# Layer 3 of a conv/attention hybrid: the output bias as a GpSimd addition to T

## The chip, the core and the metric

The kernel runs on one core of a Trainium2 chip. It is one program of 192724 instructions. Five engines work side by side: TensorE (PE; its weight loads are listed as PEld), VectorE (DVE), ScalarE (ACT), GpSimd (POOL) and SyncE (SP), which here issues most DMAs. Each takes its instructions in order, and they wait for each other through semaphores. The metric is the time of one execution on the device, in microseconds (us).

## What is computed

The input x is (4, 128, 48, 48): four images of 2304 positions and 128 channels. Five layers of work follow: a selective-scan block (layer 0), a deformable convolution (layer 1), a stack of linear attention with an expert layer (layer 2), and causal attention with another expert layer (layer 3). The change lies in the causal attention of layer 3:

```
t = _to_tokens(x)                       # (4, 2304, 128)
...
t = t + _L3_attn_ref(_ln_t(t), ...)
t = t + _L3_ffn_ref(_ln_t(t), ...)

def _L3_attn_ref(x, qkv_w, qkv_b, out_w, out_b):     # 4 heads of 32
    qkv = jnp.einsum('btc,oc->bto', x, qkv_w) + qkv_b
    q, k, v = jnp.split(qkv, 3, axis=-1)
    ...
    att = jnp.where(causal, att, -jnp.inf)
    att = jax.nn.softmax(att, axis=-1)
    out = jnp.einsum('bhqk,bhkd->bhqd', att, v)
    ...
    return jnp.einsum('btc,oc->bto', out, out_w) + out_b
```

The bias that concerns us is `out_b`, plus the part of the value bias that passes through the output weights: since the weights of a softmax sum to one, the bias of v adds `v_b @ out_w.T` to every row. The kernel forms this sum once, in `o_b`.

## The kernel before

T holds the tokens of all images in on-chip memory, [128 partitions, 4 x 18 tiles, 128 channels] in f32, and stays there from layer 1 to the end. A tile is 128 tokens; a block is three tiles (384 tokens), so an image has six blocks. The four heads are worked in two pairs, so layer 3 has 4 x 6 x 2 = 48 pieces of work, called `Block` in the code.

For each image, `normed` takes mean and variance of all 18 tiles (VectorE) and turns the variance into a factor (GpSimd, L1817). For each of its blocks, `prepare` returns seven steps: `norm` writes the normalised block xn (three VectorE instructions, L1830); `turn` transposes it (TensorE, L1842) and copies it to xT (ACT, L1844); four `project` steps make q and k for two pairs of heads (L1848, then VectorE L1854 or ACT L1850); `value` makes v (L1866, ACT L1869). `largest` takes the row maxima of the scores: score products on TensorE (L1891), on the diagonal an addition (L1900), then the maximum on VectorE (L1901); `take` transposes the maxima (L1910) and adds them to q (L1912). `scores` makes one tile row of transposed scores (L1945), its exponential on ACT (L1953), and on the last three rows of a block the causal mask on GpSimd (L1956); `weighed` multiplies it with v (L1974), three units later (UNIT_LAG). When both pairs of a block are done, `divide` runs in six steps: two empty ones, the reciprocal in two halves and the product with it (L1999, L2001), an empty one, and `output`, whose inner function `project` multiplies with the output weights (L1925), adds the bias (L1926) and adds the result to T (VectorE, L1928).

The order on TensorE, ACT, VectorE and GpSimd is the order in which the Python code calls these steps: the whole layer stands under `manual_schedule`. The main loop goes through the 48 blocks and their tile rows. In each unit it calls `scores`, then as many steps of `largest` for the following block as are due, then one step of `divide` if any is waiting (`doing`), then, in every other unit or in short blocks in each, one step of preparation (`others`), and then `weighed` for the unit three back.

Results of TensorE go to PSUM. The pool `ps` has one buffer with the tag "ps" for the transposes, q, k, v, the maxima and the output projection, so each of these waits until the one before it has been read. The scores for the maxima have one buffer too (`pa`), the transposed scores two (`pb`), the weighted sums one (`po`).

A row of ones (`env.ones_row`, one partition of 128) as weights, times a row of 128 values, writes these values to all 128 partitions. This is how L1926 adds the bias: a product with a single row behind each projection product, three times per block, into the same PSUM tile.

A similar bias addition exists in layer 2: there GpSimd adds a bias tile to three tiles of tokens (L1180), and the tile is made by one product with the row of ones and a copy.

Of the kernel before, what the change touches and what calls it, by code (L numbers as in the profile page):

```python
# [15 lines left out]
F32 = mybir.dt.float32  # L16
# [7 lines left out]
P = 128  # L24
NB = 4
C = 128
# [5 lines left out]
G3 = BLK // P  # L32
# [1715 lines left out]
def layer3(env, io, T):  # L1748

    with ExitStack() as ctx:  # L1750
        _layer3(ctx, env, io, T)
# [5 lines left out]
def _layer3(ctx, env, io, T):  # L1757
# [6 lines left out]
    nc, tc, ident = env.nc, env.tc, env.ident  # L1764
    cp = ctx.enter_context(tc.tile_pool(name="l3c", bufs=1))
# [7 lines left out]
    def load(name, shape):  # L1773
        t = cp.tile(shape, F32, name=name)
        nc.sync.dma_start(t, io[name])
        return t

    def psum(*shape):
        return ps.tile(list(shape), F32, name="ps", tag="ps")
# [4 lines left out]
    v_b = load("l3_v_b", [P, 1])  # L1784
    oT_w = load("l3_owT", [P, C])
    o_b = load("l3_ob", [1, C])
    later = load("l3_later", [P, P])

    spread = [cp.tile([P, G3, P], F32, name=f"spread{i}") for i in range(NP3)]
# [11 lines left out]
    def normed(im):  # L1801

        t = {}

        def some(g0):
            if g0 == 0:
                t["st"] = sp.tile([P, NT, nc.vector.BN_STATS_DIM], F32, name="st")
                im.mv = sp.tile([P, NT, nc.vector.BN_AGGR_DIM], F32, name="mv")
                im.rstd = sp.tile([P, NT], F32, name="rstd")
                im.q = bp.tile([P, NP3, L], F32, name="q")  # L1810
                im.k = bp.tile([P, NP3, L], F32, name="k")
            for g in range(g0, g0 + G3):
                nc.vector.bn_stats(out=t["st"][:, g, :], in_=im.T[:, g, :])
                nc.vector.bn_aggr(out=im.mv[:, g, :], in_=t["st"][:, g, :])
            if g0 + G3 == NT:
                nc.vector.tensor_scalar_add(im.rstd, im.mv[:, :, 1], 1e-5)
                nc.gpsimd.tensor_tensor(im.rstd, im.rstd, env.half[:, :NT], ALU.pow)  # L1817

        return [lambda g0=g0: some(g0) for g0 in range(0, NT, G3)]

    def prepare(im, j):

        at = bass.ts(j, BLK)
        t = {}

        def norm():
            t["xn"] = sp.tile([P, G3, C], F32, name="xn")
            for g in range(G3):
                i = j * G3 + g
                nc.vector.tensor_scalar(  # L1830
                    t["xn"][:, g, :],
                    im.T[:, i, :],
                    im.mv[:, i, 0:1],
                    im.rstd[:, i : i + 1],
                    op0=ALU.subtract,
                    op1=ALU.mult,
                )

        def turn():
            pt = psum(P, BLK)  # L1840
            for g in range(G3):
                nc.tensor.transpose(pt[:, bass.ts(g, P)], t["xn"][:, g, :], ident)  # L1842
            t["xT"] = sp.tile([P, BLK], F32, name="xT")
            nc.scalar.copy(t["xT"], pt)  # L1844

        def project(s, p):
            pq = psum(P, BLK)
            nc.tensor.matmul(pq, w_qk[:, s, p, :], t["xT"], start=True, stop=True)  # L1848
            if s:
                nc.scalar.activation(  # L1850
                    im.k[:, p, at], pq, AF.Identity, bias=b_qk[:, s, p : p + 1]
                )
            else:
                nc.vector.tensor_scalar(  # L1854
                    im.q[:, p, at],
                    pq,
                    b_qk[:, s, p : p + 1],
                    DH3**-0.5,
                    op0=ALU.add,
                    op1=ALU.mult,  # L1860
                )

        def value():
            pv = psum(P, G3, C)
            for g in range(G3):
                nc.tensor.matmul(  # L1866
                    pv[:, g, :], t["xT"][:, bass.ts(g, P)], w_v, start=True, stop=True
                )
            nc.scalar.copy(  # L1869
                im.v[:, j * G3 : (j + 1) * G3, :, :DH3],  # L1870
                pv.rearrange("p g (h d) -> p g h d", d=DH3),
            )

        return [norm, turn] + [
            lambda s=s, p=p: project(s, p) for s in range(2) for p in range(NP3)
        ] + [value]
# [44 lines left out]
    def output(im, j, oT):  # L1921
        def project():
            pp = psum(P, G3, C)
            for g in range(G3):
                nc.tensor.matmul(pp[:, g, :], oT[:, bass.ts(g, P)], oT_w, start=True, stop=False)  # L1925
                nc.tensor.matmul(pp[:, g, :], env.ones_row, o_b, start=False, stop=True)  # L1926
            dst = im.T[:, j * G3 : (j + 1) * G3, :]
            nc.vector.tensor_add(dst, dst, pp)  # L1928

        return project  # L1930
# [8 lines left out]
    def scores(x, t):  # L1939
        g0 = max(t - x.j * G3, 0)  # L1940
        cols = slice(g0 * P, BLK)
        sc = pb.tile([P, 2, 512], F32, name="scT")
        for r in range(2):
            rows = slice(r * 64, r * 64 + 64)
            nc.tensor.matmul(  # L1945
                sc[:, r, cols],
                x.im.k[rows, x.p, bass.ts(t, P)],
                x.im.q[rows, x.p, x.j * BLK + g0 * P : (x.j + 1) * BLK],
                start=True,
                stop=True,  # L1950
            )
        pT = sp.tile([P, 2, BLK], F32, name="pT", bufs=UNIT_LAG + 2)
        nc.scalar.activation(pT[:, :, cols], sc[:, :, cols], AF.Exp)  # L1953
        if t >= x.j * G3:
            own = pT[:, :, g0 * P : (g0 + 1) * P]
            nc.gpsimd.affine_select(  # L1956
                out=own,
                in_=own,
                pattern=[[0, 2], [1, P]],
                compare_op=ALU.is_ge,  # L1960
                fill=0.0,
                base=0,
                channel_multiplier=-1,
            )
        x.__dict__.setdefault("pT", {})[t] = pT
# [54 lines left out]
    def preparation(im):  # L2020
        return normed(im) + [s for j in range(NBLK) for s in prepare(im, j)]

    def run(steps):
        for s in steps:
            s()

    with tc.manual_schedule(engines=ORDERED):
        pr = psum(1, C)
        nc.tensor.matmul(pr, v_b, oT_w, start=True, stop=True)
        nc.vector.tensor_add(o_b, o_b, pr)  # L2030
        run(normed(images[0]) + prepare(images[0], 0))
        parts, take = largest(images[0], 0, 0)
        run(parts + [take])
        others = [s for j in range(1, NBLK) for s in prepare(images[0], j)]
        waiting, done, doing = [], [], []
        for i, x in enumerate(blocks):
            n = x.last + 1
            if x.j == 0 and x.p == 0 and x.im.b + 1 < NB:
                others += preparation(images[x.im.b + 1])
            following = blocks[i + 1] if i + 1 < len(blocks) else None  # L2040
            parts, take = largest(following.im, following.j, following.p) if following else ([], None)
            if following and following.im is x.im and x.im.b == 0:

                need = (NBLK - 1 - following.j) * (2 + 2 * NP3 + 1)
                need += 0 if x.im.b + 1 == NB else len(preparation(images[1]))
                while len(others) > need:
                    others.pop(0)()
            total = len(parts)
            for t in range(n):
                scores(x, t)  # L2050
                while parts and (total - len(parts)) * max(n - 1, 1) < total * (t + 1):
                    parts.pop(0)()
                if doing:
                    doing.pop(0)()
                if others and (t % 2 == 0 or n < 7):
                    others.pop(0)()
                waiting.append((x, t))
                if len(waiting) > UNIT_LAG:
                    y, s = waiting.pop(0)
                    weighed(y, s)  # L2060
                    if s == y.last and y.p == NP3 - 1:
                        doing += divide(y)
            run(parts)
            if following and following.im is not x.im:
                run(others)
                others = []
            if take:
                take()
        for y, s in waiting:
            weighed(y, s)  # L2070
            if s == y.last and y.p == NP3 - 1:
                doing += divide(y)
        run(doing)
# [155 lines left out]
```

## Time and profile before

| | |
|---|---|
| time, median of 3 runs | 12985.0 us (12982.07 to 13003.0) |
| profiled execution | 12885.25 us |
| its span (first to last instruction) | 12883.3 us |
| TensorE busy | 11151.3 us (87%) |
| VectorE busy | 8493.7 us (66%) |
| ACT busy | 6929.4 us (54%) |
| GpSimd busy | 4401.5 us (34%) |
| layer 3, from its first product to its last addition to T | 11028 to 12565 us |
| mean granted clock of TensorE | 0.935 |

How to read it: the profile lists each engine's instructions grouped by the line of the kernel that issued them and by operation. Each group gives what it writes and reads, partitions x elements, how many there are, their busy time and mean duration, and how long the engine sat idle just before them and for whom it waited. Matrix products of f32 operands are recorded as two instructions each. Products overlap in the pipeline, so that the duration of one is longer than the distance from its start to the next one's. The granted clock is the share of its full clock that TensorE was given.

### The profile page before, as it was taken

To read this page: it belongs to the slowest core of one execution; us is meant where nothing else is said; L and a number is where in the kernel's file an instruction comes from. 1 tells how busy PE (TensorE), PEld (TensorE's weight loads), DVE (VectorE), ACT (ScalarE), POOL (GpSimd) and SP (SyncE) were. 2 spreads that over 40 slices of the span, in tenths; PEclk is the share of its full clock that TensorE was granted. 3 is DMA by queue.
4 is the path that set the end of the run, shared out by engine and by line. 5 is a ranking of instruction groups with operands and counts; after the bars stand their busy time and mean duration, and the time that the engine had idled before them with its cause. 6 is when DMAs were issued, how large, how long until landed. Compare 5 with 4: busy or idle time off the path is not lost. (4 is left out here: it accounts for less than half of the span.)

```text
span 12883.3 us, 192724 instructions
## 1 busy us (share of the span) xinstructions
PE 11151.3 (87%) x71150; PEld 8431.5 (65%) x71150; DVE 8493.7 (66%) x15424; ACT 6929.4 (54%) x13281; POOL 4401.5 (34%) x4727
## 2 busy tenths in 40 slices
PE   6879788878797887689799999999999997899997
PEld 4667666766676666488677787777877774333333
DVE  4998889888988899455555666566665653444442
ACT  3777777777777777311155655555565653123322
POOL 1443333333333344277643333333333331000000
PEclk9999999999999999799899999999999997799995
DMA  2221222122212222266500000000000003000003
GB/s 104 67 71 63 77 79 71 63 77 80 71 63 75 81 67 67 85 189 197 149 1 3 3 4 2 4 3 3 4 2 3 1 1 117 10 6 7 7 8 120
DMA packets 307846, 677.49 MB, mean 53 GB/s; under 512 B 39109, under 2 KB 128985, under 8 KB 304865
## 3 DMA queue, kind: packets, MB, share of 16 engines
q1 hardware_dynamic: 254032, 493.49, 12.2%
q0 software_dynamic: 51840, 169.91, 4.7%
q8 instruction: 571, 9.36, 0.3%
q14 instruction: 363, 2.97, 0.1%
q10 hardware_dynamic: 1040, 1.77, 0.0%
HBM read 602.63 MB, written 71.85 MB: 52 GB/s over the span
## 5 line engine op out<-in xcount | busy, mean ns | idle before, releaser
L565 ACT ACTIVATE hs<-ps,bct 128x256 f32<-128x256 f32 x4608 | 1853.9, 474 | 1182.0 <-PE ps L559 1130.5
L559 PE MATMUL ps<-ident,h 128*128 128x128 f32 x9216 | 1496.1, 294 | 778.8 <-DVE h L545 608.8
L559 PEld LDWEIGHTS ps<-ident,h 128*128 128x128 f32 x9216 | 1083.0, 148 | 1162.5 <-DVE h L545 716.2
L573 PE MATMUL yp<-ident,hs 128*128 128x128 f32 x9216 | 1408.2, 289 | 28.5 <-ACT ys L588 28.5
L505 ACT ACTIVATE dA<-delta,l_Al 128x768 f32<-128x768 f32 x1536 | 1388.3, 936 | 0.3
L512 POOL TENSOR_TENSOR h<-du,rB 128x512 f32<-128x512 f32 x768 | 1077.5, 1403 | 767.5 <-PE ps L559 689.0
L573 PEld LDWEIGHTS yp<-ident,hs 128*128 128x128 f32 x9216 | 1159.9, 151 | 82.7 <-ACT ys L588 57.6
L545 DVE TENSOR_TENSOR_SCAN h<-dA,h 128x256 f32<-128x256 f32 (+1 forms) x1024 | 1083.4, 1058 | 27.2
L545 DVE TENSOR_TENSOR_SCAN h<-dA,carry,h 128x768 f32<-128x768 f32 x512 | 1027.9, 2008 | 10.6 <-ACT dA L505 10.6
L1180 POOL TENSOR_TENSOR T<-T,bias 128x384 f32<-128x384 f32 x384 | 383.8, 999 | 1560.4 <-DVE fn L1108 1520.2
L487 POOL TENSOR_SCALAR_AFFINE_SELECT dB<-bct 128x512 f32<-128x512 f32 x768 | 748.4, 975 | 385.5 <-PE b L519 244.9
L1953 ACT ACTIVATE pT<-scT 128x768 f32<-128x768 f32 (+2 forms) x504 | 377.6, 749 | 894.2 <-PE scT L1945 894.0
L519 PE MATMUL b<-dB,duT 128*128 128x128 f32 x6144 | 830.2, 279 | 0.8 <-ACT duT L445 0.8
L545 DVE TENSOR_TENSOR_SCAN h<-dA,carry,b 128x512 f32<-128x512 f32 x512 | 645.7, 1261 | 267.8 <-PE b L519 250.5
L949 POOL DMA_INDIRECT g<-table,idx x648 | 710.1, 1096 | 263.6 <-issue 146.4
L519 PEld LDWEIGHTS b<-dB,duT 128*128 128x128 f32 x6144 | 770.7, 197 | 2.4 <-POOL h L512 1.2
L962 PE MATMUL pt<-ident,gw 128*128 128x128 f32 x5184 | 661.9, 283 | 103.3 <-DVE gw L956 100.4
L956 DVE TENSOR_TENSOR gw<-g,wq 128x512 f32<-128x512 f32 x648 | 445.9, 694 | 427.9 <-DMA g<-table,idx 377.3
L962 PEld LDWEIGHTS pt<-ident,gw 128*128 128x128 f32 x5184 | 608.0, 193 | 152.1 <-DVE gw L956 119.7
L552 POOL COPY carry<-h 128x2 f32<-128x2 f32 x512 | 97.3, 190 | 1780.4 <-DVE h L545 1715.2
L1901 DVE TENSOR_REDUCE mx<-sc 128x2 f32<-128x1024 f32 (+3 forms) x400 | 428.5, 1071 | 364.8 <-PE sc L1891 359.8
L516 DVE TENSOR_TENSOR h<-du,rB 128x512 f32<-128x512 f32 x768 | 633.3, 825 | 4.2 <-DMA rB<-rows 4.1
(341 smaller groups left out, 23182.1 us busy)
## 6 DMA issues: line engine op xcount, KB each, us to landing
rB<-rows SPq DMA_DIRECT2D x768, 384.0 KB, 3.5
w<-f_w SPq DMA_DIRECT2D x64, 1024.0 KB, 6.4
table<-y SPq DMA_DIRECT2D x9, 2304.0 KB, 17.8
table<-tok SPq DMA_DIRECT2D x16, 1152.0 KB, 10.4
g<-table,idx POOLq DMA_INDIRECT x648, 3.8
xb<-x SPq DMA_DIRECT2D x48, 192.0 KB, 3.1
xn<-xn SPq DMA_DIRECT2D x48, 192.0 KB, 3.5
yd<-y SPq DMA_DIRECT2D x4, 2304.0 KB
```

What stands on the lines that cost most here:

```text
L487: nc.gpsimd.affine_select(out=x.dB[n], in_=x.bc[:, m0 : m0 + CT // P, n : n + 1].to_broadcast([P, CT // P, P]), pattern=[[0, CT // P], [1, ...
L505: nc.scalar.activation(dA, x.delta[:, d, :], AF.Exp, scale=A[:, d, x.k, n : n + 1])
L512: nc.gpsimd.tensor_mul(h[:, 1, own], x.du[:, 1, own], x.rB[n][:, own])
L516: nc.vector.tensor_mul(x.h[n][:, :, own], x.du[:, :, own], b)
L519: nc.tensor.matmul(b0[:, bass.ts(m, P)], x.duT[:, m, :], x.dB[n][:, m, :], start=True, stop=True,)
L545: nc.vector.tensor_tensor_scan(h, da, b, initial=first, op0=ALU.mult, op1=ALU.add)
L559: nc.tensor.transpose(tt[:, m, bass.ts(d, P)], x.h[n][:, d, bass.ts(2 * q + m, P)], ident)
L565: nc.scalar.activation(hs, tt[:, m, :], AF.Copy, scale=x.bc[:, 2 * q + m, NS + n : NS + n + 1])
L573: nc.tensor.matmul(yp[:, q, (2 * d + m) * P : (2 * d + m + 1) * P], hs[:, bass.ts(d, P)], ident, is_transpose=True, start=n == 0 and m == ...
L949: nc.gpsimd.indirect_dma_start(out=g, out_offset=None, in_=table, in_offset=bass.IndirectOffsetOnAxis(ap=idx[:, j : j + 1], axis=0),)
L956: nc.vector.tensor_mul(gw, g.rearrange("p (q c) -> p q c", c=C), wq[:, i, t, :].unsqueeze(2).to_broadcast([P, 4, C]),)
L962: nc.tensor.matmul(pt[:, t - t0, :], gw[:, q, :], ident, start=q == 0, stop=q == 3)
```

## The change

The 72 products with the row of ones behind the output projection go. In their place, a tile `bias` of [128, 1, 128] is filled once at the start of layer 3 (one product with the row of ones, one ACT copy), and the step `turn` of each block begins with a GpSimd addition of this tile, repeated three times, to the block's own tiles of T. The block's norm (step `norm`) has read T by then; the attention's result is added to the same tiles later, in `project`.

```diff
@@ constants of layer 3
     o_b = load("l3_ob", [1, C])
+    bias = cp.tile([P, 1, C], F32, name="bias")
     later = load("l3_later", [P, P])
@@ prepare
         def turn():
+
+            own = im.T[:, j * G3 : (j + 1) * G3, :]
+            nc.gpsimd.tensor_add(own, own, bias.to_broadcast([P, G3, C]))
             pt = psum(P, BLK)
             for g in range(G3):
                 nc.tensor.transpose(pt[:, bass.ts(g, P)], t["xn"][:, g, :], ident)
@@ output
         def project():
             pp = psum(P, G3, C)
             for g in range(G3):
-                nc.tensor.matmul(pp[:, g, :], oT[:, bass.ts(g, P)], oT_w, start=True, stop=False)
-                nc.tensor.matmul(pp[:, g, :], env.ones_row, o_b, start=False, stop=True)
+                nc.tensor.matmul(pp[:, g, :], oT[:, bass.ts(g, P)], oT_w, start=True, stop=True)
             dst = im.T[:, j * G3 : (j + 1) * G3, :]
             nc.vector.tensor_add(dst, dst, pp)
@@ start of layer 3
         nc.vector.tensor_add(o_b, o_b, pr)
+        pr = psum(P, C)
+        nc.tensor.matmul(pr, env.ones_row, o_b, start=True, stop=True)
+        nc.scalar.copy(bias[:, 0, :], pr)
         run(normed(images[0]) + prepare(images[0], 0))
```

On GpSimd's queue the 24 additions stand between the factors of the norms (L1817 of the kernel before) and the masks (L1956); those of the later blocks of an image stand between masks of earlier blocks. The instructions of the other layers are the same and in the same order.

## The prediction

> **What bounds the kernel now.** The page came first: 12883.3 us of span (12885.25 us for the profiled execution), TensorE busy 87%, and a chain of waits that is mostly TensorE with the attention of layer 3 (L1945, L1891, L1974) at its head. Then I cut layer 3 out, from its first product (11028 us) to its last addition to T (12565 us). Here are a group of the page, and after it the row of that stretch, whose columns are length, busy time of PE, PEld, DVE, ACT and POOL with instruction counts, granted clock, DMA share, GB/s.
>
> ```profile
> L1180 POOL TENSOR_TENSOR T<-T,bias 128x384 f32<-128x384 f32 x384 | 383.8, 999 | 1560.4 <-DVE fn L1108 1520.2
> ```
> ```profile
> 11028.00:12565.00 1537.00, 1385.65 (x6474) 542.58 (x6474) 723.79 (x1251) 449.57 (x649) 77.25 (x151) 0.92 0.03 7
> ```
>
> In layer 3 TensorE is busy 90% of the time, VectorE 47%, GpSimd 5%, and the clock is 0.92 of full. So work taken off TensorE counts here, if nothing takes its place. The groups by line in the same stretch:
>
> ```profile
> L1956 POOL TENSOR_SCALAR_AFFINE_SELECT pT<-pT 128x256 f32<-128x256 f32 x144 | 58.8, 408 | 1418.1 <-ACT pT L1953 1418.1
> L1926 PE MATMUL ps<-l_ob,ones_row 1*128 1x128 f32 x144 | 41.2, 372 | 0.0
> L1925 PE MATMUL ps<-l_owT,sums 128*128 128x128 f32 x144 | 40.4, 368 | 10.6 <-DVE sums L2001 8.7 <-ACT pT L1953 1.9
> L1866 PE MATMUL ps<-l_wv,xT 128*128 128x128 f32 x144 | 24.6, 312 | 2.0 <-ACT k L1850 2.0
> L1928 DVE TENSOR_TENSOR T<-T,ps 128x384 f32<-128x384 f32 x24 | 13.3, 555 | 43.0 <-PE ps L1926 43.0
> ```
>
> Each of the 24 projections has three product pairs, and each product is two instructions (144 = 24 x 3 x 2). VectorE sits idle 43.0 us ahead of the 24 additions, waiting for L1926: it has time to take T earlier. L1866 (the values) has the very form that the projection has after the change: six instructions, 128x128 weights and 128 columns each. The timeline of two such places, TensorE alone (start, length, what), a projection and then a value product:
>
> ```profile
> 12248.64 0.49 PE L1925 MATMUL ps<-l_owT,sums 128*128 128x128 f32 x2
> 12249.06 0.48 PE L1926 MATMUL ps<-l_ob,ones_row 1*128 1x128 f32 x2
> 12249.48 0.49 PE L1925 MATMUL ps<-l_owT,sums 128*128 128x128 f32 x2
> 12249.89 0.48 PE L1926 MATMUL ps<-l_ob,ones_row 1*128 1x128 f32 x2
> 12250.31 0.49 PE L1925 MATMUL ps<-l_owT,sums 128*128 128x128 f32 x2
> 12250.73 0.48 PE L1926 MATMUL ps<-l_ob,ones_row 1*128 1x128 f32 x2
> 12251.14 0.44 PE L1974 MATMUL out<-pT,v 128*64 128x128 f32 x4
> 12251.51 1.65 PE L1945 MATMUL scT<-q,k 64*128 64x384 f32 x4
> ```
> ```profile
> 12022.30 0.94 PE L1866 MATMUL ps<-l_wv,xT 128*128 128x128 f32 x6
> 12023.16 0.87 PE L1974 MATMUL out<-pT,v 128*64 128x384 f32 x4
> ```
>
> The projection holds TensorE from 12248.64 to 12251.14, 2.50 us; the value product, from start to next start, 0.86 us. And the score product behind the projection takes 1.65 us, where it takes 0.92 us at full clock. That led to the clock. The view by stretches around another projection (before it, during it, the gap behind it, the next two):
>
> ```profile
> 12001.90:12012.72 10.82, 10.82 (x50) 3.67 (x48) 7.68 (x10) 3.96 (x6) 0.00 (x0) 1.00 0.00 1
> 12012.72:12015.30 2.58, 2.57 (x14) 1.77 (x12) 1.23 (x1) 0.00 (x0) 0.00 (x0) 1.00 0.00 0
> 12015.30:12015.95 0.65, 0.01 (x1) 0.02 (x1) 0.56 (x1) 0.00 (x0) 0.00 (x0) 1.00 0.00 0
> 12015.95:12019.35 3.40, 3.40 (x8) 1.15 (x10) 0.00 (x0) 0.58 (x1) 0.00 (x0) 0.51 0.00 0
> 12019.35:12025.00 5.65, 5.65 (x34) 2.42 (x32) 1.99 (x4) 2.27 (x4) 0.81 (x2) 0.99 0.01 3
> ```
>
> Full clock, a projection, 3.4 us at half clock, full clock again. I read the clock of the whole layer in steps of 0.85 us. Of 24 falls from full to half after the warm-up, **12 begin inside a projection or within 5 us of its start**. Of 24 value products only one has a fall so near, of the 24 transposes L1842 none.
>
> **The change, part by part.**
>
> *Products removed.* By the timeline six plain instructions take 0.86 us where twelve mixed ones take 2.50: 1.64 us saved, times 24 = 39 us. The other end is half of the mixed run, 1.25 us, times 24 = 30 us: the alternation of 128-row and 1-row weights would then cost nothing of its own. I take 39, since L1866 is the same form. None of it lies beside other TensorE work.
>
> *What is late next.* The addition L1928 must follow VectorE's earlier work. Reading the 24 places one by one, VectorE is free 0.92 to 1.26 us ahead of L1928 at about half of them and 2.7 us or more at the others. Done 1.64 us earlier, the products wait up to 0.7 us for it. This counts only where TensorE's next instruction wants the one "ps" buffer (some 15 places, L1848, L1842, L1910). I sum 3 us: 39 - 3 = 36 us.
>
> *GpSimd's additions.* 24 of them, the same form as L1180: 24 x 0.999 = 24 us on an engine that is busy 77 of 1537 us. On its queue an addition stands between the masks L1956, and in `turn` it waits for the three norms L1830, which TensorE's transposes in the same step wait for as well, so the queue is held no longer than TensorE itself. Behind it stand masks, whose readers L1974 come three units later; a unit here is about 2.5 us of TensorE, so 1 us is covered. L1928 waits for an addition many us old. Cost 0; without cover, 24 us. VectorE loses nothing: L1928 has the same form.
>
> *Set-up.* One more ones-product and an ACT copy run behind the addition to o_b (11028.7). TensorE is idle until 11040.36, waiting for norms, and ACT until 11041.43; both are under 1 us and hide. No DMA is added or moved.
>
> *The clock.* Each fall costs half of its length. The 12 falls at projections cost 49 us in all, the sum of (1 - clock) over their steps. Here **a rule of the Trainium skill** speaks against any gain. "TensorE: Matmul & The Clock Gate", section "Why this matters for your kernels", says that gaps of more than about 3 us between bursts drop the clock. No gap at these falls is over 1.1 us, and at 12251 there is none, so by the rule the falls have nothing to do with the projection and the sum stays at 36 us. The trace differs: the stall of 0.65 to 1.0 us behind the transposes L1910 comes 48 times, and seven falls follow within 5 us, those after the warm-up all around a change of image, where waits are longer. A projection without any gap falls. What it alone has is half of its products with one row of weights. I take it, as an estimate, that such products count little as activity, and that after the change a projection looks to the clock like L1866. Two thirds of 49 us go, times 0.85 because at full clock some waits on VectorE come out again: 28 us. The ends are 0 and 49.
>
> Sum: 36 + 28 = 64 us, 12885 to about 12821. The median of the runs is 100 us above the profiled execution; the same difference gives 12985 - 64 = **12921 us**.
>
> **The rivals.**
>
> 1. *Forecast*: 45 to 95 us gained, 12890 to 12940. Chance 0.62.
> 2. *The products go, the clock stays as it was* (the rule above). 12985 - 36 = 12949. For it: falls also follow waits of 1.3 to 1.9 us on VectorE, and stalls of 0.65 us stay. Against it: the count of 12 to 1. Chance 0.22, nearly all of it past the mark of 0.2% (26 us, what a measurement of this kernel can tell from no change).
> 3. *GpSimd stands in the way*: masks behind it are late, or VectorE is held off memory. "SBUF — State Buffer", section "SBUF: two separate sides", has one of the two engines blocked for the other's whole instruction. Each addition on the path at full length: 36 - 24 = 12 us, 12973. Against it: 384 L1180 in layer 2 show a median of 997 ns and few waits, and VectorE's work in layer 3 mostly reads PSUM. Chance 0.10.
> 4. *Slower*: the projection, shorter and with a stall behind it, leaves TensorE less active in a window. All 24 would start a fall (12 more at 49/12 = 4.1 us), and the 12 there are would each last one step of 3.4 us longer (1.7 us each): 49 + 20 - 36 = 33 us lost, 13018. It decides from nine more falls on (36/4.1). Against it: L1866 followed by more work doesn't fall. Chance 0.06.
>
> That the bias lands wrongly or twice is excluded: the addition is ordered after the norms that read T, and each block is turned once.
>
> **How the numbers follow.** Faster by over 0.2%: case 1 and most of case 2, 0.81. Within: case 3 and the rest of 2, 0.13. Slower: case 4, 0.06. Range: down to 39 + 49 + some falls caused by waits, 12882; up to case 2 with the lower price of the products and some stalls, 12966.
>
> **What would show it.** L1926 gone but for one product; six projection instructions in about 0.86 us at full clock; the layer's stretch 1473 us or so; its clock up from 0.92 to 0.94 or more, with falls at few projections; the additions on GpSimd at 1.0 us with masks no later. It is wrong if the falls at projections stay near 12, if the six instructions keep 0.2 us each, or if waits on L1928 grow past 10 us.

## The result, and the profile after

The changed kernel takes 12921.9 us (median of 5 runs, 12900.41 to 12934.53) against 12986.56 us before (5 runs, 12982.07 to 13003.0): ratio 0.9945, 95% interval 0.993 to 0.996, or 65 us less. Timed once more in a later session the ratio was 0.9948 (0.9934 to 0.9961).

The two profiled executions seem to contradict this: 12902.88 us after, 12885.25 us before. They have to be compared by stages. From the first to the last transpose of a gathered tile (L962), layer 1 takes 911 us in the profile of before and 1003 us in that of after, though nothing of it was changed. A second profile of the kernel before has 1008 us there and 12998.65 us in all. So the stage that was changed is measured by itself: layer 3, from its first product to the end of its last addition to T. It fell from 1536.6 us to 1449.7 us, by 87 us.

The row of that stretch in the changed kernel, with columns as before:

```profile
11126.20:12576.00 1449.80, 1294.47 (x6332) 498.89 (x6332) 721.38 (x1246) 450.46 (x650) 101.43 (x175) 0.96 0.03 7
```

TensorE is busy 91 us less and its clock is 0.96 of full instead of 0.92; VectorE and ACT do what they did; GpSimd does 24 us more. The groups by line in the same stretch (the changed kernel's lines: L1929 the projection's products, L1931 the addition to T, L1843 the new additions, L1959 the masks):

```profile
L1959 POOL TENSOR_SCALAR_AFFINE_SELECT pT<-pT 128x256 f32<-128x256 f32 x144 | 59.4, 412 | 1147.4 <-ACT pT L1956 1147.3
L1929 PE MATMUL ps<-l_owT,sums 128*128 128x128 f32 x144 | 25.1, 317 | 11.3 <-DVE sums L2004 8.7 <-ACT pT L1956 2.5
L1843 POOL TENSOR_TENSOR T<-T,bias 128x384 f32<-128x384 f32 x24 | 23.9, 998 | 162.2 <-DVE xn L1831 162.2
L1931 DVE TENSOR_TENSOR T<-T,ps 128x384 f32<-128x384 f32 x24 | 13.2, 549 | 7.1 <-PE ps L1929 7.1
```

The masks wait for ACT as before, not for the additions. VectorE's idle time ahead of L1931 fell from 43.0 to 7.1 us: now it is VectorE that comes late. Here is the projection that the prediction showed in stretches (at 12012 us there), in the changed kernel: TensorE's timeline first, then the stretches (before it, during it, the gap, the next 3.4 us).

```profile
12053.20 0.94 PE L1929 MATMUL ps<-l_owT,sums 128*128 128x128 f32 x6
12055.06 0.91 PE L1852 MATMUL ps<-xT,l_wqk 128*128 128x384 f32 x2 [0.92 <-DVE T L1931]
```
```profile
12043.00:12053.20 10.20, 10.20 (x47) 3.37 (x46) 7.19 (x10) 3.83 (x5) 0.00 (x0) 1.00 0.00 1
12053.20:12054.14 0.94, 0.94 (x8) 0.74 (x6) 0.82 (x1) 0.00 (x0) 0.00 (x0) 1.00 0.06 17
12054.14:12055.05 0.91, 0.00 (x0) 0.00 (x0) 0.87 (x2) 0.00 (x0) 0.00 (x0) 1.00 0.00 0
12055.05:12058.45 3.40, 3.39 (x16) 1.23 (x16) 0.00 (x0) 1.31 (x2) 0.00 (x0) 1.00 0.00 0
```

Six instructions in 0.94 us; then a gap that is longer than before (0.91 us, formerly 0.65); and yet full clock behind it, where before 3.4 us went at half clock.

### The profile page after: what moved, and what is told of

Read it like the earlier page. It is cut to its first block, busy times and chain, and to the rows that moved or that the text cites. A ratio compares the mean times of both kernels' runs of the same rounds, so it can differ in the third digit from the quotient of the medians.

```text
span 12901.0 us, 192475 instructions
## 1 busy us (share of the span) xinstructions
PE 11084.8 (86%) x71008; PEld 8420.0 (65%) x71008; DVE 8476.0 (66%) x15424; ACT 6937.8 (54%) x13282; POOL 4373.2 (34%) x4751
## 5 line engine op out<-in xcount | busy, mean ns | idle before, releaser
L1956 ACT ACTIVATE pT<-scT 128x768 f32<-128x768 f32 (+2 forms) x504 | 378.0, 750 | 837.5 <-PE scT L1948 833.3
L962 PE MATMUL pt<-ident,gw 128*128 128x128 f32 x5184 | 676.0, 291 | 158.4 <-DVE gw L956 131.7
L949 POOL DMA_INDIRECT g<-table,idx x648 | 658.1, 1016 | 403.6 <-DVE gw L956 174.9
L962 PEld LDWEIGHTS pt<-ident,gw 128*128 128x128 f32 x5184 | 639.1, 204 | 190.1 <-DVE gw L956 127.8
```

The costliest lines, as they stand in the source:

```text
L949: nc.gpsimd.indirect_dma_start(out=g, out_offset=None, in_=table, in_offset=bass.IndirectOffsetOnAxis(ap=idx[:, j : j + 1], axis=0),)
L962: nc.tensor.matmul(pt[:, t - t0, :], gw[:, q, :], ident, start=q == 0, stop=q == 3)
```

## The experiments

Each kernel was read in the same way as in the prediction: the length of layer 3, the clock in steps of 0.85 us from 32 us after the layer's first product, the falls from full to half (the warm-up counts as one), those that begin within 5 us of a projection's start, and the clock's loss, the sum of (1 - clock) over the steps. Profiles of one kernel agree within some 5 us in the first column. Each variant was profiled once, the kernel before and the changed kernel with the later `divide` twice, the changed kernel three times.

| kernel | layer 3, us | clock's loss, us | falls | at projections |
|---|---|---|---|---|
| before | 1536.6 | 114.2 | 25 | 12 |
| before_again | 1539.7 | 119.0 | 24 | 11 |
| after | 1449.7 | 48.4 | 12 | 2 |
| after_again | 1454.9 | 59.9 | 10 | 2 |
| after5 | 1452.0 | 51.3 | 12 | 2 |
| full_rows | 1464.4 | 53.5 | 13 | 0 |
| zero_rows | 1464.5 | 54.3 | 12 | 0 |
| rows_96 | 1469.4 | 63.7 | 13 | 0 |
| ones_at_values | 1502.4 | 67.8 | 15 | 2 (and 4 at values) |
| before_late | 1479.9 | 61.9 | 12 | 1 |
| add_alone | 1533.0 | 108.8 | 24 | 13 |
| no_add | 1451.9 | 56.4 | 11 | 1 |
| late_divide | 1442.9 | 62.0 | 15 | 0 |
| late_divide5 | 1446.9 | 67.6 | 16 | 0 |

**The same kernels again** (no edit), to learn what a second profile changes.

> The kernel before, unchanged, for a second profile. Both theories: layer 3 (first product to last addition to T) repeats its 1536.6 us within 10 us, with about 12 falls of the clock at its 24 projections. If the stretch moves by 30 us or more between profiles of one kernel, the gain of 87 us in layer 3 is partly chance. What differs from the first profile should lie in layer 1, whose gathers took 911 us in the profile of before and 1003 us in that of the change.

> The changed kernel, unchanged, for a second profile. If the clock's part is real: layer 3 again 1440 to 1460 us, clock losses about 48 us, two or three falls at projections. If the first profile was luck: 1475 to 1500 us and six or more falls at projections.

Both repeat: 1539.7 and 1454.9 us (the clock's loss of the changed kernel is 59.9 us, not about 48). The gain in layer 3 is 82 to 90 us whichever profiles are paired, and the falls at projections go from 11 or 12 to 2.

**More rows in the bias product.** The kernel before, its 72 products kept, on 128 rows:

```diff
-                nc.tensor.matmul(pp[:, g, :], env.ones_row, o_b, start=False, stop=True)
+                nc.tensor.matmul(pp[:, g, :], even, bias[:, 0, :], start=False, stop=True)
```

where `even` is [128, 128] of 1/128 and `bias` holds the bias in every row.

> The kernel before with the 72 bias products kept in place, but with 128 rows of weights (all 1/128) against 128 rows that each hold the bias: as many products of the same columns, all rows of the array at work. Theory (few rows count as little activity for the clock): falls at projections drop from 12 to 4 or fewer and layer 3 takes 1470 to 1500 us. And if mixing 1-row with 128-row weights costs time of its own, the twelve instructions take 1.7 us at full clock, not 2.5 us. Rival (the length of the projection or its many small weight loads cause the falls, not the rows): 10 or more falls at projections remain, layer 3 at 1525 to 1545 us.

The theory's side, and 6 us beyond its range: the 12 instructions are still there, no fall is left at a projection, and 74 of the 86 us come without removing any product. The same projection in this kernel, as timeline and then in stretches (before it, during it, the gap, the next 3.4 us):

```profile
12074.02 0.49 PE L1928 MATMUL ps<-l_owT,sums 128*128 128x128 f32 x2
12074.35 0.39 PE L1929 MATMUL ps<-bias,even 128*128 128x128 f32 x2
12074.57 0.39 PE L1928 MATMUL ps<-l_owT,sums 128*128 128x128 f32 x2
12074.79 0.39 PE L1929 MATMUL ps<-bias,even 128*128 128x128 f32 x2
12075.02 0.39 PE L1928 MATMUL ps<-l_owT,sums 128*128 128x128 f32 x2
12075.24 0.39 PE L1929 MATMUL ps<-bias,even 128*128 128x128 f32 x2
```
```profile
12063.30:12074.02 10.72, 10.72 (x48) 3.58 (x49) 7.67 (x10) 3.86 (x6) 0.00 (x0) 1.00 0.00 1
12074.02:12075.63 1.61, 1.61 (x14) 1.41 (x12) 1.23 (x1) 0.00 (x0) 0.00 (x0) 1.00 0.00 0
12075.63:12076.27 0.64, 0.00 (x0) 0.00 (x0) 0.56 (x1) 0.00 (x0) 0.00 (x0) 1.00 0.00 0
12076.27:12079.67 3.40, 3.40 (x16) 1.24 (x16) 0.00 (x0) 1.31 (x2) 0.00 (x0) 1.00 0.02 5
```

Starts are 0.22 us apart, where the pairs with one row were 0.42 us apart; the twelve take 1.54 us to the next instruction where none waits, before 2.50 us. The gap behind is the same 0.64 us, and the clock stays full.

Two kernels vary this. In `zero_rows` the 128 rows are there, but all except the first are zeros:

> The kernel before with 128-row bias products in which only the first row of weights (ones) and of the moving operand (the bias) is not zero, the other 127 rows are zeros. If it is the rows that an instruction takes up that count for the clock: as with all rows filled, no more than two falls at projections, layer 3 at 1455 to 1475 us. If it is the data that change: 8 or more falls, layer 3 at 1500 us or more (the twelve instructions still at about 1.5 us).

In `rows_96` the product runs on 96 rows:

```diff
+                nc.tensor.matmul(pp[:, g, :], even[:96, :], bias[:96, 0, :], start=False, stop=True)
```

> The kernel before with the bias products on 96 rows (weights 1/96) in place of one. If every product that changes the number of rows costs the slow pace, the twelve instructions take 2.5 us as before; if only the single row does, 1.5 to 1.7 us. With 2.5 us the clock tells the causes apart: no more than 3 falls at projections and 1475 to 1500 us for layer 3 if few active rows make it fall; 8 or more falls and 1525 us or more if it is the slow pace of the products and the gap behind them.

Zeros make no difference (1464.5 us, no falls at projections): it is the rows that an instruction takes up, not the data. 96 rows go at the quick pace (1.54 us where nothing waits) and no falls come at projections. The second half of that expectation, which was to separate the rows from the slow pace, therefore had no chance to speak: the two came and went together.

**The one-row products elsewhere.** In the changed kernel, the bias of v is added by one-row products at the values:

```diff
                 nc.tensor.matmul(
-                    pv[:, g, :], t["xT"][:, bass.ts(g, P)], w_v, start=True, stop=True
+                    pv[:, g, :], t["xT"][:, bass.ts(g, P)], w_v, start=True, stop=False
                 )
+                nc.tensor.matmul(pv[:, g, :], env.ones_row, v_row, start=False, stop=True)
```

where `v_row` holds the bias of v as a row; `bias` then holds `out_b` alone.

> The changed kernel, with the bias of the values added by three products with the row of ones behind the three value products of each block (72 in all), and left out of the output's bias. So the one-row products stand at another place, where before hardly a fall was seen. Theory (few rows): the value product takes 2.5 us in place of 0.86 and 8 or more falls come within 5 us of the 24 value products; layer 3 takes 1510 to 1540 us. Rival (it is the place: the projection with its stall behind it): at most 3 falls at the value products, layer 3 at 1485 to 1495 us, which is the 1450 us plus 24 x 1.64 us of product time.

Between the two: the slow pace came along (2.50 us for the twelve), but only 4 falls, and 1502 us. One-row products alone bring few falls. What the values lack is the gap: the next instruction doesn't use the one buffer, and at 23 of the 24 places TensorE goes on at once.

**The gap taken away.** The kernel before, with `divide` called later in its unit:

```diff
-                if doing:
-                    doing.pop(0)()
                 if others and (t % 2 == 0 or n < 7):
                     others.pop(0)()
                 ...
                     if s == y.last and y.p == NP3 - 1:
                         doing += divide(y)
+                if doing:
+                    doing.pop(0)()
```

> The kernel before, ones products kept, with the step of divide called behind the weighed product in its unit, so that the next user of the one buffer no longer stands right behind the projection and the gap of 0.65 us goes. Theory A (one-row products alone make the clock fall): 8 or more falls at the 24 projections, layer 3 at 1520 to 1535 us, by the gaps alone. Theory B, formed after the run with the ones products at the values showed only 4 falls there (one-row products and a gap behind them in the same stretch make it fall): at most 4 falls, layer 3 at 1480 to 1505 us.

Theory B: one fall, 1479.9 us. The one-row products are still there at their slow pace, and 58 us are gained (against the mean of the two profiles of before, 1538 us), some 8 of which are the gaps themselves (13 of 0.65 us). The move shifts the other steps of `divide` as well; what that alone is worth wasn't tried. The kernel before, as it stands, says the same: 10 of its 14 projections with a gap behind them have a fall, 2 of the 10 without.

The same projection, in stretches (before it, during it, the next 3.4 us; there is no gap):

```profile
11970.00:11980.49 10.49, 10.49 (x49) 3.59 (x49) 7.56 (x11) 3.82 (x5) 0.00 (x0) 1.00 0.04 11
11980.49:11983.00 2.51, 2.51 (x16) 1.78 (x14) 0.55 (x1) 0.00 (x0) 0.00 (x0) 1.00 0.00 0
11983.00:11986.40 3.40, 3.40 (x17) 1.24 (x16) 1.78 (x2) 1.39 (x2) 0.00 (x0) 1.00 0.00 0
```

**GpSimd's additions**, taken out of the changed kernel (which then leaves out the bias) and put alone into the one before.

> The changed kernel without the 24 additions on GpSimd: the output's bias is left out of T. My theory (the additions are covered): layer 3 at 1445 to 1460 us, as with them (1450 and 1455 us). Rival (an addition holds up masks or VectorE): 10 to 24 us less than with them, 1430 to 1440 us.

> The kernel before with 24 additions of a tile of zeros on GpSimd put in at the same place, and all products with the row of ones kept. My theory: layer 3 at 1530 to 1545 us, as before (1537 and 1540 us), 10 to 13 falls at projections. Rival (additions cost): 1550 to 1565 us.

Without them 1451.9 us, within the 1449.7 to 1454.9 us with them; alone 1533.0 us, not more than before. They cost nothing that shows beside 5 us from profile to profile; 24 us would.

**Both.** The changed kernel with the later `divide`:

> The changed kernel with the same move of divide. About ten projections have a gap of 0.6 to 1.3 us behind them in the changed kernel; with the weighed product in it the gap goes: layer 3 at 1435 to 1445 us under both theories of the clock, against 1450 and 1455 us. If VectorE or the one buffer merely makes TensorE wait one step later: 1450 us or more.

> The changed kernel with the step of divide behind the weighed product, timed. From the profiles (layer 3 at 1443 us against 1450 and 1455 us of the changed kernel and 1537 and 1540 us before): 85 to 100 us less than before, ratio 0.9925 to 0.9935, and 7 to 12 us less than the changed kernel on the same chip. If the shorter layer 3 is given back in the experts behind it, only 75 to 85 us.

> The changed kernel again, timed on the same chip as the former: ratio 0.993 to 0.995 to the kernel before, that is 65 to 90 us; layer 3 in its profile at 1445 to 1460 us, 1 to 3 falls of the clock at projections.

Layer 3 takes 1442.9 and 1446.9 us, 3 to 12 us less than the changed kernel's profiles, and TensorE goes on at once behind each projection but the last. The falls are no fewer (15 and 16). In the time of the whole the gain doesn't show, and the forecast for `late_divide5` failed: 60 us less than before, not 85 to 100, ratio 0.9939 (0.9925 to 0.9953) against 0.9948 (0.9934 to 0.9961) on the same chip, with medians of 12925.49 and 12917.75 us. Its experts behind layer 3 take 328 and 338 us in the two profiles, the changed kernel's 319 to 325 us, so that in these profiles what layer 3 gains is given back there. The clock's loss in these experts is larger too, 139 and 157 us against 129 to 134 us; why, wasn't tried. Whether it is the better kernel stays open.

## Why the prediction was right, and where not

- *The bound.* Right: with TensorE busy 90% of layer 3, what left its path left the time.
- *The products* (36 us). Right for the projection itself. From the projection's start to the next instruction that waits for nothing it went from 2.50 to 0.87 us, 1.63 x 24 = 39 us. The value product was the right row to price it by; half of the mixed run (1.25 us) was not, and `full_rows` says why: a change between 128 rows and one takes time. The twelve instructions have five such changes, (2.50 - 1.54)/5 = 0.19 us each. How much of the 36 us reached the time isn't shown by itself (see the clock).
- *What is late next* (3 us). Right: TensorE's waits for the addition behind a projection are up to 0.60 us longer, some 3 to 4 us in all.
- *GpSimd at nothing, set-up hidden.* Right within 5 us; `no_add` and `add_alone` show the first. The copy to `bias` took 0.27 us at the start, while TensorE waited for the norms.
- *The clock* (28 us). Right in kind, and the term of the sum that was mis-sized. The loss fell from 114 and 119 us to 48 to 60 us, by 63 us in the means; at the factor of 0.85 that is 54 us, not 28. Two thirds of the falls at projections was too few: 12 became 2, and in the first profile of the changed kernel these two begin within 0.11 us of a projection's start, too early to be its doing. And falls beside them were shorter: in the kernel before three that cost 5.1 us each (10.24 us at half clock) began just ahead of a projection (11135, 11238, 12272) and held on through it; the changed kernel's first profile has one such, at 11961.75, that costs 3.4 us. 36 + 54 = 90 us, measured 82 to 90. But the factor of 0.85 was never measured: at its full amount the clock's 63 us would leave 23 of the mean gain of 86 us for the products.
- *The rule on gaps.* It was read as if shorter gaps did nothing. Gaps of over 3 us aren't needed: 0.65 us was enough behind one-row products, and 0.91 us was not behind full ones. Rival 2, built on that reading, is refuted. Two readings beside it were wrong: two of the twelve falls (11538 and 11914) begin within 0.4 us of a projection's start, behind a wait of 1.9 us ahead of it, not under 1.1 us; and six of the 48 stalls behind L1910 last 1.5 to 4.1 us. The other ten falls carry the argument.
- *The cause of the falls.* Half right. That one-row products are the matter is shown by `full_rows`, `zero_rows` and `rows_96`. But I took one projection without a gap (12251) as proof that they suffice, and `before_late` shows that they rarely do: without the gap, 1 fall in 23. Nor does it take both. By the traces it is the sum that counts, one-row products and idle time within one window of 3.4 us (the last section). Whether the one-row products themselves count as nothing there, or the whole mixed run as half, isn't settled.
- *Rivals 3 and 4.* The additions hold up nothing, and the shorter projections have fewer falls, not more.
- *The total.* 12921 us forecast, 12921.9 us measured, and closer than its terms deserve: layer 3 gained 86 us, not 64, but the medians differ by 65. The experts behind layer 3 took 319 to 325 us in the three profiles of the changed kernel, 317 and 319 us before, so some 4 us were given back. The rest lies within what the other layers vary: from layer 2's last product to layer 3's first it took 294 to 318 us in the profiles of the changed kernel, and the interval of the ratio reaches from 52 to 91 us.

## What to carry to other kernels

A bias row added by a product with a row of ones can cost TensorE more than its own instructions: here each change between 128 rows and one took 0.19 us, and together with a short wait behind such products the clock often fell to half for 3.4 us or a multiple of it. Where such a product has to stay, give it more rows (96 rows of 1/96 did about as well as 128; nothing between 1 and 96 was tried), or put work that needs no freed buffer behind it; where another engine is idle, add the bias there. And read the granted clock in steps of about a microsecond around each kind of work before you price its removal: here it was, by the estimates above, more than half of the gain.

## What the runs showed that I had not expected

- The clock has a grid of its own. In each of the 14 profiles, every change of the granted clock lies within 2 ns of a grid of 3.4133 us that runs through the whole execution, and every stretch at half clock is one or more of its windows long. The projection at 12012 again, in the kernel before, by three windows of this grid:

```profile
12012.60:12016.01 3.41, 2.76 (x15) 1.85 (x13) 1.78 (x2) 0.06 (x1) 0.00 (x0) 1.00 0.00 0
12016.02:12019.42 3.40, 3.40 (x8) 1.15 (x10) 0.00 (x0) 0.58 (x1) 0.00 (x0) 0.50 0.00 0
12019.43:12022.84 3.41, 3.41 (x20) 1.44 (x19) 1.78 (x3) 1.18 (x2) 0.41 (x1) 1.00 0.02 5
```

A fall goes with how little TensorE did in the window before. Count the time in which its products stream: 0.111 us per recorded instruction of 128 columns (the distance of the value product's starts at full clock), in proportion for other widths, cut off where the next one starts. Of the windows at full clock in layer 3, from 32 us after its first product, in all 14 profiles:

| windows | followed by half clock | of these, under 0.39 streaming | followed by full clock | of these, under 0.39 streaming |
|---|---|---|---|---|
| without one-row products | 163 | 154 | 5020 | 4 |
| with them, counted as nothing | 37 | 33 | 131 | 1 |
| with them, counted like the rest | 37 | 3 | 131 | 0 |
| with them, the whole mixed run as half | 37 | 37 | 131 | 8 |

So idle time and the slow pace don't explain the falls by themselves: the products with one row, or the whole run in which they stand, count for less than their time. The share of 0.39 was found in these traces, and no kernel was built to test it. It also says where luck enters: which projections have a fall depends on where the grid happens to lie.

- The distance of starts is the same 0.111 us in the value product and among the full-row products of `full_rows`; with one row and 128 rows in turn it is 0.20 to 0.21 us.
- Layer 1 takes about 905 us (901 to 911) in five of the profiles and about 1005 us (1003 to 1014) in the others, whichever the kernel, and the same for all profiles of a session. The three later sessions ran on three different chips, so that the chip may be the cause. A span of one profile against that of another would have given the changed kernel as 18 us slower.
